# LSTM grid and landmark attention on one core: where the twice-normed rows are added up, and how the first statistics are loaded

## The chip, the cores and the metric

The kernel runs on one core of a Trainium2 chip. The metric is the device time of one execution in microseconds (us), the median over three runs. The engines are PE (TensorE: matmuls and turns by an identity, with PEld its weight loads), DVE (VectorE), ACT (ScalarE), POOL (GpSimd) and SP (SyncE, which issues most DMAs here). Each engine takes its instructions in order.

## The reference, cut to what matters

```
x: 16 images x 64 x 64 cells x 128 features
g = group norm of x over a whole image (32 groups of 4 features)
two-dimensional LSTM over g: cell (i, j) needs h and c of (i-1, j) and (i, j-1)
    f0 = sigmoid(g wf0 + h_up uf0)      f1 = sigmoid(g wf1 + h_left uf1)
    it, ot = sigmoid(..), cp = tanh(g wc + (h_up + h_left) uc)
    c = f0 c_up + f1 c_left + it cp ;   h = ot tanh(c)
x = x + h                                       # tokens t = 4096 rows of 128 per image
attention on layernorm(layernorm(t)): its 64 landmarks are means over 64 successive tokens
    (that is, over one grid row i of an image), of the twice-normed rows
then an output projection, a batch-normed recurrence over tokens, residuals
```

## The kernel before, in words

**group_stats** reads every image of x once (L56, 2 MB each, three buffers, from SP's queue), turns 128x128 blocks on PE (L61), and DVE takes the statistics of each feature over the tokens (L62, L63). Two small matmuls (L68, L75) join the groups, and POOL makes grstd with a power (L28, L29). In front of it in PE's queue are the matrices of the attention's convolution (L637 to L640), which need cb_tm, a DMA from a scratch tensor in DRAM.

**lstm_grid** walks the 127 antidiagonals d of the 64x64 grid: all cells (i, d-i) of one diagonal are independent. Features lie on partitions in the gates; one column is one cell of one image. The 16 images are two halves of 8. A *unit* is a diagonal (up to 32 cells, both halves together, at most 512 columns) or, for diagonals with more cells, one half of it. There are 190 units, and *slot* t of the program works on unit t and, in a software pipeline, on its neighbours:
- load (L182, SP's queue) for unit t+5: x rows in *tiles* of up to 16 cells x 8 images = 128 rows, tokens on partitions
- gate_h for unit t (five gates: L207 on PE, L209 on ACT); gate_x for unit t+1 (L203)
- measure for t-2 (L226, L227 on DVE), then the cell: L288 on DVE, L289 on POOL (forget gate times cell), L290 to L292, tanh L293 on ACT
- turn for t-1: h is turned to tokens (hq, L218) and x is added (L220, into ls_tt); h of unit t is made at L297, and the sum of neighbours for the coming diagonal at L199
- factors for t-2 on POOL (L235 to L241, two of them powers)
- enter for t+2: x is turned to features (xp, L189), mean off (L192 DVE), grstd on (L195 POOL)
- normalise for t-3 (L246 on ACT) writes the twice-normed rows, tokens on partitions, into the upper half of ls_tt; store (L253, SP) writes the rows to DRAM
- collect for t-4: the twice-normed rows are turned back to features (yq, L259) and added into acc, laid out features x grid row x image (L261).

The order on all five engines is the program's own (manual schedule). The tiles of a diagonal are cut from its first cell lo, so the last tile is a partial one. PSUM has 8 banks: five for the gates (z) and one each for xp, hq and yq.

**landmarks** then scales acc by gamma/64 and adds beta (L489), and projects it.

Of the kernel before, what the change touches and what calls it, by code (L numbers as in the profile page):

```python
# [8 lines left out]
F32 = mybir.dt.float32  # L9
# [6 lines left out]
P = 128  # L16


STEPS = 32
HALF = STEPS // 2  # L20
EPS = 1e-5


# [8 lines left out]
def group_stats(nc, tc, x, ident, mhalf, gmean, grstd):  # L32

    B, D0, D1, F = x.shape
    N = D0 * D1
    K = N // P
    GS = 4
    with ExitStack() as ctx:
        cp = ctx.enter_context(tc.tile_pool(name="gs_c", bufs=1))
        ld = ctx.enter_context(tc.tile_pool(name="gs_ld", bufs=3))  # L40
        sp = ctx.enter_context(tc.tile_pool(name="gs_s", bufs=2))
        ps = ctx.enter_context(tc.tile_pool(name="gs_ps", bufs=4, space=PSUM))
        ps1 = ctx.enter_context(tc.tile_pool(name="gs_ps1", bufs=1, space=PSUM))

        avg = cp.tile([P, P], F32, name="gs_avg")
        nc.gpsimd.memset(avg, 1.0 / GS)
        for base, sign in ((0, 1), (GS - 1, -1)):
            nc.gpsimd.affine_select(
                out=avg, in_=avg, compare_op=ALU.is_ge, fill=0.0, base=base,
                pattern=[[-GS * sign, P // GS], [0, GS]], channel_multiplier=sign,  # L50
            )

        mv = cp.tile([P, B, 2], F32, name="gs_mv")
        for b in range(B):
            xb = ld.tile([P, K, F], F32, tag="xb", name="gs_xb")
            nc.sync.dma_start(out=xb, in_=x[b].rearrange("i j f -> (i j) f").rearrange("(p k) f -> p k f", k=K))  # L56
            st = sp.tile([P, K // 4, 6], F32, tag="st", name="gs_st")
            for q in range(K // 4):
                tp = ps.tile([P, 4, P], F32, tag="tp", name="gs_tp")
                for k in range(4):  # L60
                    nc.tensor.transpose(tp[:, k, :], xb[:, 4 * q + k, :], ident)  # L61
                nc.vector.bn_stats(st[:, q, :], tp.rearrange("p k n -> p (k n)"))  # L62
            nc.vector.bn_aggr(mv[:, b, :], st.rearrange("p q s -> p (q s)"))  # L63

        mean = cp.tile([P, B], F32, name="gs_mean")
        nc.vector.tensor_copy(mean, mv[:, :, 0])
        mg = ps1.tile([P, B], F32, tag="mg", name="gs_mg")
        nc.tensor.matmul(mg, avg, mean, start=True, stop=True)  # L68
        nc.vector.tensor_copy(gmean, mg)
        dev = cp.tile([P, B], F32, name="gs_dev")  # L70
        nc.vector.tensor_sub(dev, mean, gmean)
        nc.vector.tensor_mul(dev, dev, dev)
        nc.vector.tensor_add(dev, dev, mv[:, :, 1])
        vg = ps1.tile([P, B], F32, tag="vg", name="gs_vg")
        nc.tensor.matmul(vg, avg, dev, start=True, stop=True)  # L75
        var = cp.tile([P, B], F32, name="gs_var")
        nc.vector.tensor_copy(var, vg)
        inv_std(nc, cp, grstd, var, mhalf, "gs")


def lstm_tiles(nc, cp, shape, w, u, bias):
# [21 lines left out]
    rows = [cp.tile([P, KT, 2 * F + 4], F32, name=f"ls_tt{k}") for k in range(7)]  # L103
    for a in rows:
        nc.vector.memset(a[:, :, F : F + 4], 1.0)
    return wt, ut, bt, hs, cs, rows


def lstm_grid(nc, tc, x, fixed, ident, mhalf, gmean, grstd, t1, acc):

# [6 lines left out]
    T = P // HB  # L119
    NC = D0 * HB  # L120
    KT = NC // P
    AHEAD = 5
    xv = x.rearrange("b i j f -> (i j) b f")
    tv = t1.rearrange("b n f -> n b f")
    with ExitStack() as ctx:
        ld = ctx.enter_context(tc.tile_pool(name="ls_ld", bufs=AHEAD + 4, reuse_waits="tile"))
        wk = ctx.enter_context(tc.tile_pool(name="ls_wk", bufs=2, reuse_waits="tile"))
        sm = ctx.enter_context(tc.tile_pool(name="ls_sm", bufs=4, reuse_waits="tile"))
        ps_z = ctx.enter_context(tc.tile_pool(name="ls_psz", bufs=5, space=PSUM, reuse_waits="tile"))
        ps_t = ctx.enter_context(tc.tile_pool(name="ls_pst", bufs=1, space=PSUM, reuse_waits="tile"))  # L130

        wt, ut, bt, hs, cs, rows = fixed

        class Unit:
            pass
# [1 line left out]
        def unit(t, d, s0, s1):  # L137
# [3 lines left out]
            v.n = v.hi - v.lo  # L141
            v.len = v.n * HB
            v.cols = v.ns * v.len

            runs = [(s, i, min(T, v.hi - i)) for s in range(s0, s1) for i in range(v.lo, v.hi, T)]
            runs = [r for r in runs if r[2] == T] + [r for r in runs if r[2] < T]
            v.tiles = [(k, *r) for k, r in enumerate(runs)]
            whole = sum(r[2] == T for r in runs)
# [7 lines left out]
            hp, hn = hs[(d + 1) % 2], hs[d % 2]  # L156
            before, now = cs[(d + 1) % 2], cs[d % 2]
            v.hu, v.hl, v.ho = part(hp, v.lo), part(hp, v.lo + 1), part(hn, v.lo + 1)
            v.cu, v.cl, v.co = part(before, v.lo), part(before, v.lo + 1), part(now, v.lo + 1)
            v.tt = rows[t % len(rows)]  # L160
            v.z, v.a = {}, {}
# [5 lines left out]

        def span(v, s, i, c):

            return slice((s - v.s0) * v.len + (i - v.lo) * HB, (s - v.s0) * v.len + (i - v.lo + c) * HB)  # L170

        def at(v, s, i, c):
            r = v.d + (D1 - 1) * i
            return slice(r, r + (D1 - 1) * (c - 1) + 1, D1 - 1), slice(s * HB, s * HB + HB)

        def norm(v, a):
            return a[:, v.s0 * HB : v.s1 * HB].rearrange("p (s b) -> p s b", b=HB)[:, :, None, :].to_broadcast([P, v.ns, v.n, HB])

        def load(v):
            v.xt = ld.tile([P, KT, F], F32, tag="xt", name="ls_xt")  # L180
            for k, s, i, c in v.tiles:
                nc.sync.dma_start(out=v.xt[: c * HB, k, :], in_=xv[at(v, s, i, c)])  # L182

        def enter(v):

            xp = ps_t.tile([P, NC], F32, tag="xp", name="ls_xp")
            for k, s, i, c in v.tiles:
                q = c * HB
                nc.tensor.transpose(xp[:, span(v, s, i, c)], v.xt[:q, k, :], ident[:q, :q])  # L189
            v.xn = wk.tile([P, NC], F32, tag="xn", name="ls_xn", bufs=4)[:, : v.cols]  # L190
            a = v.xn.rearrange("p (s c b) -> p s c b", s=v.ns, b=HB)
            nc.vector.tensor_tensor(  # L192
                a, xp[:, : v.cols].rearrange("p (s c b) -> p s c b", s=v.ns, b=HB), norm(v, gmean), ALU.subtract
            )
            nc.gpsimd.tensor_tensor(a, a, norm(v, grstd), ALU.mult)  # L195

# [15 lines left out]
        def turn(v):  # L212

            hq = ps_t.tile([P, KT, P], F32, tag="hq", name="ls_hq")
            for k, s, i, c in v.tiles:
                q = c * HB
                j = (i - v.lo) * HB
                nc.tensor.transpose(hq[:q, k, :], v.ho[:, s - v.s0, j : j + q], ident)  # L218
            for q, k0, k1 in v.parts:
                nc.vector.tensor_add(v.tt[:q, k0:k1, 0:F], hq[:q, k0:k1, :], v.xt[:q, k0:k1, :])  # L220

# [7 lines left out]
        def factors(v):  # L229
# [6 lines left out]
            nc.gpsimd.tensor_scalar(ve[:, 1, :k], var, 1.0 + EPS, EPS * EPS, ALU.mult, ALU.add)  # L236
            nc.gpsimd.tensor_tensor(v.tt[:, 0:k, F + 2], ve[:, 0, :k], mhalf[:, :k], ALU.pow)  # L237
            nc.gpsimd.tensor_tensor(v.tt[:, 0:k, F + 3], ve[:, 1, :k], mhalf[:, :k], ALU.pow)  # L238
            v.nb = sm.tile([P, KT], F32, tag="nb", name="ls_nb")
            nc.gpsimd.tensor_tensor(v.nb[:, :k], mean, v.tt[:, 0:k, F + 3], ALU.mult)  # L240
            nc.gpsimd.tensor_scalar(v.nb[:, :k], v.nb[:, :k], -1.0, None, ALU.mult)  # L241
# [8 lines left out]

        def store(v):
            for k, s, i, c in v.tiles:
                nc.sync.dma_start(out=tv[at(v, s, i, c)], in_=v.tt[: c * HB, k, :])  # L253

        def collect(v):
            yq = ps_t.tile([P, NC], F32, tag="yq", name="ls_yq")
            for k, s, i, c in v.tiles:
                q = c * HB
                nc.tensor.transpose(yq[:, span(v, s, i, c)], v.tt[:q, k, F + 4 :], ident[:q, :q])  # L259
            ar = acc[:, v.lo : v.hi, v.s0 * HB : v.s1 * HB].rearrange("p c (s b) -> p s c b", b=HB)  # L260
            nc.vector.tensor_add(ar, ar, yq[:, : v.cols].rearrange("p (s c b) -> p s c b", s=v.ns, b=HB))  # L261

        units, ready = [], {-1: []}
        for d in range(D0 + D1 - 1):
# [48 lines left out]
        with tc.manual_schedule(  # L313
# [2 lines left out]
                mybir.EngineType.SP,  # L316
            }
        ):
            nc.vector.memset(acc, 0.0)
            for t in range(AHEAD):  # L320
                load(units[t])
            for t in range(2):
                enter(units[t])
            for r in ready[-1]:
# [26 lines left out]
def landmarks(nc, tc, acc, gamma, beta, wqkv, mask, ident, qm, km, pinvT):  # L351
# [19 lines left out]
    with ExitStack() as ctx:  # L371
# [113 lines left out]
        with tc.manual_schedule(  # L485
            engines={mybir.EngineType.PE, mybir.EngineType.DVE, mybir.EngineType.Activation, mybir.EngineType.Pool}
        ):
            for w in range(B // GI):
                nc.vector.tensor_scalar(  # L489
                    xl[w], acc[:, :, images(w)].rearrange("p i b -> p b i"), gm, beta, ALU.mult, ALU.add  # L490
                )
            project_queries(0)
            project_keys(0)
# [904 lines left out]
def kernel(ctx: ExitStack, tc: tile.TileContext, ins: dict, out: bass.AP):  # L1398
# [25 lines left out]
    with tc.tile_pool(name="at_c", bufs=1) as ac, tc.tile_pool(name="at_x", bufs=1) as xp, tc.tile_pool(  # L1424
# [6 lines left out]
        qm = lmk.tile([P, B, 2, D0], F32, name="qm")  # L1431
        km = lmk.tile([P, B, 2, D0], F32, name="km")
        with tc.tile_pool(name="first", bufs=1) as first:
            acc = first.tile([P, D0, B], F32, name="acc")
            gmean = first.tile([P, B], F32, name="gmean")
            grstd = first.tile([P, B], F32, name="grstd")
            lw = [[ins[f"L0_conv_{k}{g}"] for g in GATES] for k in "wub"]
            with tc.tile_pool(name="ls_c", bufs=1) as lc:
                lstm_fixed = lstm_tiles(nc, lc, (B, D0, F), *lw)
                with tc.manual_schedule(engines={mybir.EngineType.SP}):  # L1440
                    group_stats(nc, tc, x, ident, mhalf, gmean, grstd)
                lstm_grid(nc, tc, x, lstm_fixed, ident, mhalf, gmean, grstd, t1, acc)
            rows = [load_rows(nc, xp, t1, 0, g) for g in range(3)]
            landmarks(nc, tc, acc, gamma, beta, wqkv, mask, ident, qm, km, pinvT)
        attention(
# [27 lines left out]
```

## Time and profile before

| | us |
|---|---|
| median of three runs | 4086.14 |
| lowest and highest | 4075.14, 4089.61 |
| profiled execution: its time | 4091.27 |
| its span, first to last instruction | 4089.7 |
| conv matrices, statistics and start of the grid | 0 to 132 |
| the grid, from the first gate_h to the last unit's | 132 to 1517 |
| landmarks, attention, recurrence | from 1529 |

| engine | busy us | share of span |
|---|---|---|
| PE | 3870.2 | 95% |
| DVE | 2983.5 | 73% |
| POOL | 2809.3 | 69% |
| ACT | 2519.4 | 62% |

The busy shares are means over stages with different limits: the second half of the span (attention and recurrence) is not touched by the change. What it touches lies in the first 1530 us, so the profile is read there, window by window. A busy PE is modelled and need not be a PE at its peak; the start times of its instructions tell more. A line of a timeline is: start, duration, engine, source line, operation, tiles, and in brackets the idle time before it with what ended it.

### The profile page before, as it was taken

The page shows a single profiled execution, that of the slowest core. Times are in us where ns is not written, and L with a number is a line of the kernel's source. Part 1 is how long each engine was busy: PE and PEld are TensorE (multiplying, and loading weights), DVE is VectorE, ACT ScalarE, POOL GpSimd, SP SyncE. Part 2 cuts the span into 40 slices and gives each one's busy share as a digit, 9 for nine tenths or more (in the row PEclk, how much of TensorE's full clock was granted, in tenths as well). Part 3 has the DMA queues.
Part 4 walks back from the last instruction along what each step waited for, and adds up shares of the span by engine and source line. Part 5 has one row for each costly group of instructions (what it writes and reads, how often), then busy time and mean ns, then how long its engine had stood idle before and what let it go on. Part 6 is the DMA issues. An engine that isn't in the chain of part 4 may idle for free. (4 is left out here: it accounts for less than half of the span.)

```text
span 4089.7 us, 99565 instructions
## 1 busy us (share of the span) xinstructions
PE 3870.2 (95%) x37526; PEld 2621.9 (64%) x37526; DVE 2983.5 (73%) x7408; ACT 2519.4 (62%) x5101; POOL 2809.3 (69%) x4189
## 2 busy tenths in 40 slices
PE   6899999999999998879999999999999999988697
PEld 4767665555567578846666666666666666655476
DVE  7678777777778775435887878877877787857465
ACT  0366655555566664335777777777767776755597
POOL 0477777777777773317888888888888888877133
PEclk9799999999999989979999999999999999989798
DMA  8122222223233220111333333333333333223799
GB/s 314 61 71 79 77 77 74 80 79 84 75 81 83 70 57 4 39 27 52 94 90 88 88 94 89 88 91 94 92 83 91 93 90 85 83 65 92 235 263 180
DMA packets 493557, 383.85 MB, mean 94 GB/s; under 512 B 35208, under 2 KB 466192, under 8 KB 491024
## 3 DMA queue, kind: packets, MB, share of 16 engines
q1 hardware_dynamic: 471680, 341.17, 28.8%
q0 software_dynamic: 17728, 34.61, 4.7%
q8 instruction: 299, 4.90, 0.5%
q10 hardware_dynamic: 3664, 1.65, 0.1%
q14 instruction: 186, 1.52, 0.1%
HBM read 172.82 MB, written 204.48 MB: 92 GB/s over the span
## 5 line engine op out<-in xcount | busy, mean ns | idle before, releaser
L209 ACT ACTIVATE ls_g<-ls_z,ls_b 128x304 f32<-128x304 f32 (+26 forms) x950 | 510.1, 548 | 401.1 <-PE ls_z L207 364.2
L931 POOL TENSOR_TENSOR at_total<-at_total,at_e 128x512 f32<-128x512 f32 x480 | 611.4, 1274 | 118.3 <-ACT at_e L904 87.2
L203 PE MATMUL ls_z<-ls_xn,ls_w 128*128 128x304 f32 (+26 forms) x1900 | 612.0, 470 | 0.0
L203 PEld LDWEIGHTS ls_z<-ls_xn,ls_w 128*128 128x128 f32 x1900 | 342.7, 197 | 176.0 <-issue 79.5
L798 POOL TENSOR_SCALAR at_T<-at_T,at_nb 128x128 f32<-128x128 f32 x512 | 403.7, 797 | 13.3
L867 DVE TENSOR_REDUCE at_mxq<-at_bank 128x1 f32<-128x512 f32 x512 | 327.7, 683 | 82.9 <-PE at_bank L864 82.6
L207 PE MATMUL ls_z<-ls_hsum,ls_u 128*128 128x304 f32 (+26 forms) x1140 | 372.5, 464 | 0.0
L289 POOL TENSOR_TENSOR ls_g<-ls_g,ls_cell 128x304 f32<-128x304 f32 (+26 forms) x190 | 175.8, 925 | 280.2 <-ACT ls_g L209 250.8
L904 ACT ACTIVATE at_e<-at_bank 128x512 f32<-128x512 f32 x512 | 264.3, 603 | 115.8 <-PE at_bank L898 112.7
L986 DVE TENSOR_REDUCE at_cmx<-at_bank 128x8 f32<-128x512 f32 x512 | 317.4, 683 | 18.5 <-PE at_bank L979 12.7
L1015 ACT ACTIVATE at_eT<-at_bank 128x512 f32<-128x512 f32 x512 | 264.3, 603 | 75.1 <-PE at_bank L1012 75.0
L207 PEld LDWEIGHTS ls_z<-ls_hsum,ls_u 128*128 128x128 f32 x1140 | 214.8, 198 | 128.6 <-issue 78.0
L246 ACT ACTIVATE ls_tt<-ls_tt,ls_nb 128x128 f32<-128x128 f32 (+9 forms) x632 | 261.0, 479 | 4.1 <-POOL ls_nb L241 4.1
L207 PE MATMUL ls_z<-ls_h,ls_u 128*128 128x304 f32 (+26 forms) x760 | 260.3, 466 | 1.7 <-DVE ls_h L297 1.6
L290 DVE TENSOR_TENSOR ls_g<-ls_g,ls_g 128x304 f32<-128x304 f32 (+26 forms) x190 | 98.3, 518 | 195.4 <-POOL ls_g L289 194.2
L237 POOL TENSOR_TENSOR ls_tt<-ls_ve,mhalf 128x4 f32<-128x4 f32 (+2 forms) x190 | 228.5, 1203 | 15.2
L1286 DVE SCALAR_TENSOR_TENSOR rc_y<-rc_w,rc_scale,rc_z 128x256 f32<-128x256 f32 x344 | 155.2, 480 | 108.5 <-PE rc_z L1273 105.7
L1273 PE MATMUL rc_z<-rc_y,rc_vT 128*128 128x256 f32 x688 | 185.4, 406 | 41.6 <-ACT rc_y L1294 29.9
L1067 ACT ACTIVATE at_z<-at_u,at_nb,at_r 128x128 f32<-128x128 f32 x512 | 211.7, 505 | 11.9 <-POOL at_nb L1062 11.9
L238 POOL TENSOR_TENSOR ls_tt<-ls_ve,mhalf 128x4 f32<-128x4 f32 (+2 forms) x190 | 214.6, 1129 | 0.0
L1077 ACT COPY at_fx<-at_bank 128x512 f32<-128x512 f32 x128 | 133.1, 1040 | 126.5 <-DVE wx_stats L1075 100.9
L1267 POOL DMA_DIRECT2D out_dram<-rc_tt x64 | 77.4, 1209 | 189.5 <-ACT rc_tt L1264 186.7
(250 smaller groups left out, 9620.6 us busy)
## 6 DMA issues: line engine op xcount, KB each, us to landing
t<-ls_tt SPq DMA_DIRECT2D x392, 130.0 KB
at_T<-t SPq DMA_DIRECT2D x128, 264.0 KB
gs_xb<-in_x_dram SPq DMA_DIRECT2D x16, 2048.0 KB
at_xh<-t SPq DMA_DIRECT2D x128, 256.0 KB
t<-at_u SPq DMA_DIRECT2D x128, 256.0 KB
out_dram<-at_u SPq DMA_DIRECT2D x128, 256.0 KB
wx<-at_fx SPq DMA_DIRECT2D x128, 256.0 KB
rc_w<-wx SPq DMA_DIRECT2D x64, 512.0 KB
```

Source lines behind the costliest of these rows:

```text
L203: nc.tensor.matmul(v.z[g][:, : v.cols], wt[g], v.xn, start=True, stop=False)
L207: nc.tensor.matmul(view(v, v.z[g]), ut[g], hin, start=False, stop=True)
L209: nc.scalar.activation(a[:, : v.cols], v.z[g][:, : v.cols], AF.Tanh if g == 4 else AF.Sigmoid, bias=bt[g])
L237: nc.gpsimd.tensor_tensor(v.tt[:, 0:k, F + 2], ve[:, 0, :k], mhalf[:, :k], ALU.pow)
L238: nc.gpsimd.tensor_tensor(v.tt[:, 0:k, F + 3], ve[:, 1, :k], mhalf[:, :k], ALU.pow)
L246: nc.scalar.activation(v.tt[:q, k, F + 4 :], v.tt[:q, k, 0:F], AF.Identity, bias=v.nb[:q, k : k + 1], scale=v.tt[:q, k, F + 3 : F + 4],)
L798: nc.gpsimd.tensor_scalar(x[:, c, :], x[:, c, :], gr.nbt[:, 0, c : c + 1], gr.nbt[:, 1, c : c + 1], ALU.mult, ALU.subtract)
L867: nc.vector.tensor_reduce(gr.im.mxq[:, n : n + 1, gr.g], gr.s[n], AX.X, ALU.max)
L904: nc.scalar.activation(gr.e[:, n].rearrange("p c m -> p (c m)"), s[n], AF.Exp)
L931: nc.gpsimd.tensor_tensor(total, total, e[:, :, c, :], ALU.add)
L986: nc.vector.tensor_reduce(gr.mx[:, n].rearrange("p j c -> p c j"), gr.s[n].rearrange("p (c j m) -> p c j m", c=C, j=2), AX.X, ALU.max)
L1015: nc.scalar.activation(gr.eT[:, n], s[n], AF.Exp)
```

## The change

- collect no longer turns anything: it adds the twice-normed rows, tokens on partitions, into acc, which is now laid out token row x half x block of 16 grid rows x feature. One DVE instruction per part of a unit replaces the yq turns and the old addition. landmarks turns acc once, eight 128x128 blocks, before L489.
- For that a token row must always stand for the same grid row, so tiles are cut at multiples of 16 cells (base) instead of from lo. From diagonal 64 on, the first tile of a unit can then hold dead rows in front. Their x rows are set to zero on POOL before the load (one memset per such tile), and their second factor is multiplied by a column of a 0/1 matrix (later) on POOL. The other tiles are whole. The number of tiles and DMAs stays as it was.
- The bank of yq goes to the gates: six z banks.
- group_stats loads quarters of an image (512 KB, eight buffers, 64 DMAs) instead of whole images (three buffers, 16 DMAs).
- The pool of x rows (ls_ld) is opened ahead of group_stats, and the rows of the first five units are loaded from ACT's queue. The memset of acc moves ahead too.

```
 group_stats:
-            xb = ld.tile([P, K, F], F32, tag="xb", name="gs_xb")
-            nc.sync.dma_start(out=xb, in_=x[b]...)
+                if q % 2 == 0:
+                    xb = ld.tile([P, 8, F], F32, tag="xb", name="gs_xb")
+                    nc.sync.dma_start(out=xb, in_=rows[:, 4 * q : 4 * q + 8, :])
...
 unit:
+            v.base = v.lo // T * T
-            runs = [... for i in range(v.lo, v.hi, T)]
+            runs = [... for i in range(v.base, v.hi, T)]
...
 load:
+                rows, cells = inner(v, i, c)
+                if rows.start:
+                    nc.gpsimd.memset(v.xt[:, k, :], 0.0)
-                nc.sync.dma_start(out=v.xt[: c * HB, k, :], in_=xv[at(v, s, i, c)])
+                eng.dma_start(out=v.xt[rows, k, :], in_=xv[cells, s * HB : s * HB + HB])
...
 factors:
+            for j, s, i, c in v.tiles:
+                if i < v.lo:
+                    f = v.tt[:, j, F + 3 : F + 4]
+                    nc.gpsimd.tensor_tensor(f, f, later[:, v.lo - i : v.lo - i + 1], ALU.mult)
...
 collect:
-            yq = ps_t.tile([P, NC], F32, tag="yq", name="ls_yq")
-            for k, s, i, c in v.tiles:
-                q = c * HB
-                nc.tensor.transpose(yq[:, span(v, s, i, c)], v.tt[:q, k, F + 4 :], ident[:q, :q])
-            ar = acc[:, v.lo : v.hi, v.s0 * HB : v.s1 * HB].rearrange(...)
-            nc.vector.tensor_add(ar, ar, yq[:, : v.cols].rearrange(...))
+            for q, k0, k1 in v.parts:
+                i = v.tiles[k0][2] // T
+                a = acc[:q, v.s0 : v.s1, i : i + (k1 - k0) // v.ns, :]
+                y = v.tt[:q, k0:k1, F + 4 :].rearrange("p (s t) f -> p s t f", s=v.ns)
+                nc.vector.tensor_tensor(a, a, y, ALU.add)
...
 start of the grid:
-                load(units[t])
+                load(units[t], nc.scalar)
...
 landmarks:
+                p = ps.tile([P, W, P], F32, tag="bank", name="lm_bank")
+                for i in range(W):
+                    nc.tensor.transpose(p[:, i, :], acc[:, w, i, :], ident)
```

## The prediction

> **What bounds the kernel now.** I read the stages first (busy time by window), then the PE timeline inside one unit of the grid, then POOL's waits by stage, last the front. Columns of the first view: window, its length, busy us (instructions) of PE, weight load, DVE, ACT, POOL, then granted clock, DMA share, GB/s.
>
> ```profile
> core 0: us, PE busy (x) PEld busy (x) DVE busy (x) ACT busy (x) POOL busy (x), PEclk, DMA share, GB/s
> ...
> 34.00:119.00 85.00, 76.19 (x512) 55.36 (x512) 84.14 (x154) 1.28 (x1) 0.00 (x0) 1.00 0.83 328
> 119.00:132.00 13.00, 4.46 (x19) 4.00 (x19) 2.12 (x11) 0.00 (x0) 3.72 (x4) 0.54 0.02 6
> ...
> 552.00:837.00 285.00, 285.00 (x994) 158.07 (x993) 213.16 (x560) 164.57 (x310) 201.94 (x250) 1.00 0.29 78
> ...
> 1145.00:1321.00 176.00, 176.00 (x784) 127.87 (x783) 140.82 (x430) 113.96 (x243) 137.01 (x214) 1.00 0.30 81
> ...
> 1446.00:1512.00 66.00, 64.33 (x427) 57.27 (x426) 57.81 (x222) 45.98 (x135) 57.27 (x127) 0.98 0.24 66
> ```
>
> The statistics (34 to 119) run at DVE's pace, 84 of 85 us. The grid (132 to 1512) shows PE full, and the timeline says this is real: gates of 416 columns start every 0.35 us, and the three groups of turns follow without a gap:
>
> ```profile
> 604.80 0.60 PE L218 MATMUL ls_hq<-ident,ls_h 128*128 128x128 f32 x4
> 605.24 0.67 PE L189 MATMUL ls_xp<-ident,ls_xt 128*128 128x128 f32 x4
> 605.84 0.71 PE L259 MATMUL ls_yq<-ident,ls_tt 128*128 128x128 f32 x4
> 606.48 0.62 PE L203 MATMUL ls_z<-ls_xn,ls_w 128*128 128x416 f32 x1
> ```
>
> Start to start, the hq turns take 0.44, the xp turns 0.60, the yq turns 0.64 us of an 8.8 us unit. But POOL and DVE are not far behind. All that POOL idles is its wait at L289 for the forget gate (us in total, times, longest), here in 552 to 837, 1145 to 1321 and 1446 to 1512:
>
> ```profile
> POOL ls_g L289 <- ACT ls_g L209: 68.2, 31, 2.5
> ```
> ```profile
> POOL ls_g L289 <- ACT ls_g L209: 28.0, 27, 1.5
> ```
> ```profile
> POOL ls_g L289 <- ACT ls_g L209: 1.7, 5, 0.6
> ```
>
> So POOL has over 2 us to spare in each unit of the first, 1.0 in the second, and nothing in the last, where POOL, not PE, sets the pace.
>
> **The change, part by part.**
>
> *yq turns removed (632).* Busy time of L259's tile by window is 11.65 (173 to 336), 17.73 (336 to 552), 19.73, 22.64 (837 to 1145), 14.65, 8.89 (1321 to 1446) and 7.40. The pipeline's last 0.1 us of each unit overlaps the next gate (0.71 against 0.64), so PE's queue loses 9.2, 14.4, 16.6, 19.1, 12.0, 7.3 and 5.8 us. *Whole tiles from diagonal 64 on:* xp turns with a remainder tile take 0.60, four whole ones as hq 0.44; summed over those units about 4.4, 3.9 and 2.3 us more in 837 to 1145, 1145 to 1321 and 1321 to 1446. PE alone would gain about 95 us. What is late next is POOL's L289 and DVE's L290 behind it.
>
> *collect on DVE.* L261 (median 0.52, one input in PSUM) becomes one addition of 256, 384 or 512 elements, plus one for a remainder below diagonal 64. By L290 (0.59 at 416 elements) and L291 (0.42 at 256) that is 0.42, 0.56 or 0.69, and 0.2 for the remainder. DVE gets 0.1 to 0.3 us more in a unit; from diagonal 64 on L220 pays half of it back (two instructions of 0.74 become one of 0.69). DVE's waits at L290 and L288 are 33.7 us in 33 units of 336 to 552: this hides it.
>
> *What that addition does to POOL.* Both inputs now lie in SBUF. The rows:
>
> ```profile
> 604.69 0.59 DVE L290 TENSOR_TENSOR ls_g<-ls_g,ls_g 128x416 f32<-128x416 f32 x1 [1.25 <-POOL ls_g L289]
> ```
> ```profile
> 604.74 0.63 POOL L235 TENSOR_SCALAR ls_ve<-ls_tt 128x4 f32<-128x4 f32 x1
> ```
> ```profile
> 1496.09 0.22 POOL L235 TENSOR_SCALAR ls_ve<-ls_tt 128x2 f32<-128x2 f32 x1
> ```
> ```profile
> 599.96 0.55 DVE L261 TENSOR_TENSOR acc<-acc,ls_yq 128x392 f32<-128x392 f32 x1
> ```
> ```profile
> 600.35 1.07 POOL L195 TENSOR_TENSOR ls_xn<-ls_xn,grstd 128x416 f32<-128x416 f32 x1
> ```
>
> L235 is 0.41 us longer when it starts under L290, and ends just behind it; L195 under the old L261 is as long as anywhere. The Trainium skill ("SBUF — State Buffer", section Who interferes with whom) has the rule: a DVE instruction with two SBUF inputs contends with a GpSimd instruction that reads SBUF, not with one that only writes it, and the later one waits for the other's end. It speaks against this change: the addition now holds back L240, L241 and L195, which start 0.1 to 0.3 us into it today. Each is then some 0.2 to 0.5 us later in a unit (length of the addition, less that start, less 0.13 for what overlaps). By the rule POOL loses 0.3 to 0.4 in most units; without it the sum below would be 16 us better. The row agrees, so I take the rule.
>
> *Dead rows.* 120 tiles (one in most units of diagonals 64 to 94, two after) get a memset of 128x128 on POOL and a multiplication of 128x1. POOL's memsets of that size in the prologue took 0.20; the nearest row to the other is L240, 0.19, and 0.28 to the next start. I take 0.47 a tile, 0.94 a unit after diagonal 94; ends 0.3 (the memset covered by handover) and 1.3 (both held back 0.41 as L235 was). SP's load now waits for the memset; behind it are only the stores of L253, some 4 us later, and SP issues 5.4 of 8.8 us, so this is free while the memset is less than that late. The first reader of a load is five units away.
>
> *Units' balance.* Gain is the smaller of PE's saving and POOL's idle less what it is given:
> - 132 to 336: +7. The narrow units up to 205 have no POOL idle: lock costs 1; the rest gets PE's saving.
> - 336 to 552: idle 1.0, lock 0.37, PE 0.44: the first few units fall short, +11.
> - 552 to 837: idle 2.3: all, +17. 837 to 1145: idle 2.1, lock 0.42, dead 0.47: all, +23.
> - 1145 to 1321: idle 0.95 without handover, less 0.3 and 0.47: 0.15 in each of 27, +4 (PE offers 16).
> - 1321 to 1446: idle 1.6, less 0.37 and 0.94: +2.5.
> - 1446 to 1512: no idle, 16 units, 0.2 and up to 0.94 more: -14 (the last five load nothing any more).
> Sum: 51 us less. The last units' factors chain pays 1.5 more behind 1512.
>
> *Sixth z bank:* nothing; the fifth gate function ends at 605.6, before the next x gates start at 606.48. The first to refill are long read.
>
> *Front.* PE's first work waits for cb_tm, which shares the DMA engines with the first three images:
>
> ```profile
> 24.07 0.77 PE L637 MATMUL cb_t<-cb_turn,cb_tm 128*128 128x128 f32 x2 [24.07 <-DMA cb_tm<-cb_flat]
> ```
> ```profile
> 127.31 0.58 PE L189 MATMUL ls_xp<-ident,ls_xt 8*128 8x8 f32 x2 [5.21 <-DMA ls_xt<-in_x_dram]
> ...
> 129.71 1.46 PE L203 MATMUL ls_z<-ls_xn,ls_w 128*128 128x16 f32 x6
> ```
>
> Three images are 6.3 MB; eight quarters are 4.2. At 0.42 MB a us, what the DMA view shows in most slices from 7 to 22 us, the queue is dry 5 us earlier: -5 (ends 0, if cb_tm needs its 17 us anyway, and -9). 48 more issues of 0.33 us on SP lie under the stage. DVE's 128 statistics are not shortened; a stage that DVE fills gains nothing from quarters. acc's memset only moves on DVE. Then x rows of the first units are loaded by ACT's queue (10 issues, ACT idle) long before: the wait to 127.31 goes, and the first gates follow grstd (125.74) and one L192 and L195 at about 126.3 instead of 129.71: -3.4. The clock is at half there either way (0.54 in 119 to 132).
>
> *End.* Eight turns at half clock, some 0.25 each, mostly under the wait for the last store to land (1528.7), and xl is then read from PSUM at a like price: +0.5, ends 0 and 2.
>
> Sum: -51 - 5 - 3.4 + 1.5 + 0.5 = -57. The profiled execution took 4091.3 (span 4089.7), 5 above the median 4086.1; the difference is taken from the median: 4029.
>
> **The rivals.**
> A. *PE gets nearly all.* The lock costs nothing (67 by the same balance) and the memsets slip into handovers (4 more): with front and end, 6.4, that is -77: 4009. For it: busy PE everywhere. Against: L235's row.
> B. *POOL becomes the bound from diagonal 64 on: slower.* If memset and multiplication are both held back behind DVE (1.3 to 1.4 a tile), POOL's idle of 837 to 1446 is overdrawn: by the same balance, at 1.4, 837 to 1145 gives 9, 1145 to 1321 -22, 1321 to 1446 -20, the narrow end -39; the rest gives 35, front and end 6.4: 31 slower, 4117. It breaks even near 1.1 a tile. Against: the memset only writes.
> C. *Little comes through.* POOL pays 0.9 a tile, by the same balance: the grid gains 14, with front and end 20: 4066, or some us more if cb_tm gains nothing (4071). Against it stands the 0.20 of the prologue's memsets.
>
> **How the numbers follow.** Likeliest 4029 (0.57), A 0.21, C 0.13, B 0.09. A difference of 0.5% (20 us) is about what a measurement of this kernel can tell. Faster 0.78, same 0.13, slower 0.09. The range runs from A with its best front (3996) to C (4072).
>
> **What would show it.** Right: units near 600 at 8.1 us instead of 8.8; L195 lengthened under L261's successor; POOL without idle after 1145; units of the narrow end longer by 0.6 to 1.0; cb_tm at about 19; first gates 8 us earlier. Wrong: units near 1200 shortened by PE's full 0.6 to 0.9 (A), units near 900 not shortened (B), cb_tm still at 24.

## The result, and the profile after

| us | before | after |
|---|---|---|
| median (lowest to highest) | 4087.88 (4075.14 to 4095.67), 4 runs | 4020.82 (4017.51 to 4027.51), 4 runs |
| profiled execution, its span | 4091.27, 4089.7 | 4021.31, 4019.8 |

The ratio is 0.9841, with a 95% interval of 0.9813 to 0.9869: 67 us less. In the two profiles the grid's last unit starts its first gate_h at 1516.6 and at 1445.3, so 71.3 us are won before that point, and 1.4 are lost behind it.

Most lines moved; the ones used below, before to after: load L182 to L200, with the new memset L199; xp turn L189 to L207; L192 to L210; L195 to L214; gate_x L203 to L222; gate_h L207 to L226; hq turn L218 to L237; factors L235 to L238 now L254 to L257, with the new multiplication L261; L240, L241 to L263, L264; addition of collect L261 to L284; L289 and L290 to L312 and L313.

To see where the 71 us are, one grid has to be laid on the other. A unit is the same stretch of the grid in both, so the table counts units (0 to 189 in the order of the program) and takes a stage from the first gate_h of one unit to that of another. "My step" is the prediction's amount for the window nearest to the stage; their ends lie up to 8 us apart.

| stage | before | after | gain | my step |
|---|---|---|---|---|
| up to the first gate_h | 131.9 | 123.4 | 8.5 | 8.4 |
| units 0 to 32 | 204.7 | 194.0 | 10.7 | 7 |
| 32 to 63 | 207.4 | 196.7 | 10.6 | 11 |
| 63 to 95 | 290.1 | 273.4 | 16.7 | 17 |
| 95 to 130 | 310.8 | 288.1 | 22.7 | 23 |
| 130 to 157 | 176.5 | 169.1 | 7.4 | 4 |
| 157 to 173 | 128.1 | 122.8 | 5.3 | 2.5 |
| 173 to 189, the narrow end | 67.2 | 77.8 | -10.6 | -14 |

The stages' busy times after the change (window, its length, busy us and instructions of PE, weight load, DVE, ACT, POOL, then granted clock, DMA share, GB/s) are the statistics, the wait for the grid, units 63 to 95, units 130 to 157, and the narrow end:

```profile
core 0: us, PE busy (x) PEld busy (x) DVE busy (x) ACT busy (x) POOL busy (x), PEclk, DMA share, GB/s
26.00:111.00 85.00, 69.59 (x501) 56.46 (x497) 83.30 (x154) 0.00 (x0) 0.32 (x2) 0.98 0.93 356
111.00:123.40 12.40, 5.47 (x34) 4.80 (x33) 5.39 (x16) 1.28 (x1) 3.72 (x4) 0.74 0.01 4
...
514.00:787.50 273.50, 273.50 (x895) 148.45 (x894) 225.65 (x605) 168.81 (x320) 218.49 (x264) 1.00 0.30 82
...
1075.60:1244.80 169.20, 165.00 (x705) 119.57 (x704) 140.61 (x404) 105.14 (x241) 156.11 (x271) 1.00 0.31 84
...
1367.50:1445.30 77.80, 63.28 (x387) 55.52 (x387) 58.95 (x226) 46.15 (x139) 69.86 (x186) 0.95 0.20 56
```

PE is still full in units 63 to 95, with 895 instructions recorded, but it is no longer full at the end (165.0 of 169.2, then 63.3 of 77.8). POOL's busy time has grown from 57.3 in 66 us to 69.9 in 77.8. The timeline of PE inside one unit shows what went: two groups of turns, and then the next gates.

```profile
570.22 2.26 PE L226 MATMUL ls_z<-ls_hsum,ls_u 128*128 128x416 f32 x6
572.31 0.60 PE L237 MATMUL ls_hq<-ident,ls_h 128*128 128x128 f32 x4
572.75 0.68 PE L207 MATMUL ls_xp<-ident,ls_xt 128*128 128x128 f32 x4
573.35 3.76 PE L222 MATMUL ls_z<-ls_xn,ls_w 128*128 128x416 f32 x10
```

POOL's waits (us in total, times, longest) have shrunk from 70.4 us (68.2 of them for ACT) to 38.9 in units 63 to 95:

```profile
POOL ls_g L312 <- ACT ls_g L228: 25.6, 20, 1.5
POOL ls_g L312 <- DMA t<-ls_tt: 13.3, 10, 1.5
```

From unit 130 to 157 the same view lists no wait of POOL at all, where it had 28.0 us before. PE, which never waited for POOL in a group of the old page, now does so in L222's: 8.0 us over the kernel.

```profile
L222 PE MATMUL ls_z<-ls_xn,ls_w 128*128 128x304 f32 (+26 forms) x1900 | 607.2, 468 | 8.6 <-POOL ls_xn L214 8.0
```

The front came out as two separate gains. The first turn of cb_tm starts 5.5 us earlier (18.61 instead of 24.07), and the x turn ahead of the first gates (that of unit 1; the one of unit 0 is not among the records) now waits for DVE's L210 and no longer for a DMA:

```profile
18.61 0.76 PE L662 MATMUL cb_t<-cb_turn,cb_tm 128*128 128x128 f32 x2 [9.09 <-DMA cb_tm<-cb_flat]
```
```profile
120.84 0.39 PE L207 MATMUL ls_xp<-ident,ls_xt 16*128 16x16 f32 x2 [3.91 <-DVE ls_xn L210]
121.19 2.32 PE L222 MATMUL ls_z<-ls_xn,ls_w 128*128 128x16 f32 x10
```

### The profile page after: what moved, and what is told of

The parts are those of the page before. It is cut to its first block, busy times and chain, and to the rows that moved or that the text cites. A ratio compares the mean times of both kernels' runs of the same rounds, so it can differ in the third digit from the quotient of the medians.

```text
span 4019.8 us, 98633 instructions
## 1 busy us (share of the span) xinstructions
PE 3774.1 (94%) x36902; PEld 2552.7 (64%) x36902; DVE 3017.4 (75%) x7408; ACT 2494.2 (62%) x5101; POOL 2910.2 (72%) x4431
## 5 line engine op out<-in xcount | busy, mean ns | idle before, releaser
L228 ACT ACTIVATE ls_g<-ls_z,ls_b 128x304 f32<-128x304 f32 (+26 forms) x950 | 489.3, 545 | 234.3 <-PE ls_z L226 200.6
L222 PE MATMUL ls_z<-ls_xn,ls_w 128*128 128x304 f32 (+26 forms) x1900 | 607.2, 468 | 8.6 <-POOL ls_xn L214 8.0
L222 PEld LDWEIGHTS ls_z<-ls_xn,ls_w 128*128 128x128 f32 x1900 | 340.6, 196 | 190.7 <-issue 85.1
L226 PE MATMUL ls_z<-ls_hsum,ls_u 128*128 128x304 f32 (+26 forms) x1140 | 371.3, 463 | 0.0
L226 PEld LDWEIGHTS ls_z<-ls_hsum,ls_u 128*128 128x128 f32 x1140 | 213.5, 196 | 128.6 <-issue 76.9
L226 PE MATMUL ls_z<-ls_h,ls_u 128*128 128x304 f32 (+26 forms) x760 | 260.7, 466 | 17.4 <-DVE ls_h L320 17.2
L316 ACT ACTIVATE ls_g<-ls_cell 128x304 f32<-128x304 f32 (+26 forms) x190 | 93.3, 491 | 284.0 <-DVE ls_cell L315 281.0
L312 POOL TENSOR_TENSOR ls_g<-ls_g,ls_cell 128x304 f32<-128x304 f32 (+26 forms) x190 | 182.5, 960 | 96.7 <-ACT ls_g L228 66.9
L256 POOL TENSOR_TENSOR ls_tt<-ls_ve,mhalf 128x4 f32<-128x4 f32 (+2 forms) x190 | 224.5, 1181 | 15.2
L313 DVE TENSOR_TENSOR ls_g<-ls_g,ls_g 128x304 f32<-128x304 f32 (+26 forms) x190 | 98.5, 518 | 159.7 <-POOL ls_g L312 155.5
L226 PEld LDWEIGHTS ls_z<-ls_h,ls_u 128*128 128x128 f32 x760 | 141.6, 196 | 110.5 <-issue 51.0
```

Of the source, the lines that this page charges most:

```text
L222: nc.tensor.matmul(v.z[g][:, : v.cols], wt[g], v.xn, start=True, stop=False)
L226: nc.tensor.matmul(view(v, v.z[g]), ut[g], hin, start=False, stop=True)
L228: nc.scalar.activation(a[:, : v.cols], v.z[g][:, : v.cols], AF.Tanh if g == 4 else AF.Sigmoid, bias=bt[g])
```

## The experiments

The work behind the grid is the same in all kernels, yet from the last unit's gate_h to the end of the span it took between 2551 us (no_sum) and 2579 us (quarters) in the profiled executions. Totals of single kernels therefore scatter by more than most parts of this change are worth, and the parts are read from the stages. Within the grid, from unit 7 to 173, a stage that an edit doesn't touch repeats within 0.7 us, and mostly within 0.1. The narrow end does so less well, because the granted clock falls to half around its last two units, in each profile at another moment: those two took 8.7 us in the changed kernel and 9.3 before, at half clock for the most part, and 5.6 to 7.2 us in four runs that kept full clock longer (turns_back, no_dead, mask_add, mask_pool).

**quarters: only the load in quarters, on the old grid.**

```diff
-        ld = ctx.enter_context(tc.tile_pool(name="gs_ld", bufs=3))
+        ld = ctx.enter_context(tc.tile_pool(name="gs_ld", bufs=8))
...
+                if q % 2 == 0:
+                    xb = ld.tile([P, 8, F], F32, tag="xb", name="gs_xb")
+                    nc.sync.dma_start(out=xb, in_=rows[:, 4 * q : 4 * q + 8, :])
```

> The kernel before, with the group statistics loaded in quarters of an image (eight buffers) and nothing else changed. If the front's gain comes from the shorter queue ahead of cb_tm and the rest from the early x rows (my steps: 5 and 3.4 us), the first cb transpose moves from 24 to about 19 us, the first gate_h from 131.9 to about 127, and the total is 5 us less. If the queue does not matter and the x rows carry all of it, cb moves too but the first gate_h stays within 1 us of 131.9. The grid itself (132 to 1517) should not move by more than 1 us, unless the earlier start also moves the moment at which TensorE's clock comes back to full; then units 0 to 7 are up to 4 us shorter.

The first cb transpose moved to 20.20, the last turn of the statistics from 117.6 to 113.1, and the first gate_h from 131.9 to 126.9: 5.0 us. Units 0 to 7 took 33.1 instead of 37.3 us. All stages from unit 7 to 173 stood still. The median was 4085.5, ratio 0.9992 (0.9983 to 1.0001): the 9 us that the grid's start won in the profile are not seen in the whole. The part behind the grid was 6 us longer in this profile; why the medians of 20 and 45 runs lie only 2.4 us apart is open.

**whole_front: quarters, and the first x rows loaded early on ACT's queue.**

```diff
-        def load(v):
+        def load(v, eng=nc.sync):
...
-            nc.vector.memset(acc, 0.0)
             for t in range(AHEAD):
-                load(units[t])
+                load(units[t], nc.scalar)
...
-            with tc.tile_pool(name="ls_c", bufs=1) as lc:
+            with tc.tile_pool(name="ls_c", bufs=1) as lc, tc.tile_pool(name="ls_ld", bufs=AHEAD + 4) as ld:
+                nc.vector.memset(acc, 0.0)
```

> The kernel before with both parts of the front: quarters, and the x rows of the first five units loaded early on ACT's queue (pool of the rows opened ahead of the statistics, accumulator cleared earlier). The grid is the old one. Theory: first gate_h at about 123.4 as in the changed kernel, units 0 to 7 at 33 us instead of 37.3, so 12 to 13 us less in all, near 0.997 of the time before. Rival (the 4 us in units 0 to 7 belong to the new grid, not to the start): units 0 to 7 stay at 37, total 8 to 9 us less. What is left to the grid is the measured 70 us less this.

First gate_h at 121.4, units 0 to 7 in 33.4 us, the last unit 13.75 us earlier; 4076.0, ratio 0.9977 (0.9968 to 0.9985), which is 6 to 13 us of the whole. So in the profiles the front is worth nearly 14 us and the new grid the other 57 or 58. What shortens units 0 to 7 is the clock. From 121 to 160 us, in the kernel before, with quarters, and with the whole front, the windows read (the granted clock is the third number from the end):

```profile
121.00:160.00 39.00, 31.89 (x146) 29.37 (x147) 12.81 (x65) 11.38 (x38) 14.18 (x34) 0.50 0.05 15
```
```profile
121.00:160.00 39.00, 36.28 (x187) 33.32 (x187) 16.53 (x79) 14.92 (x50) 15.41 (x43) 0.57 0.06 18
```
```profile
121.00:160.00 39.00, 38.70 (x213) 35.58 (x214) 20.51 (x96) 18.80 (x62) 19.57 (x52) 0.63 0.05 15
```

The granted clock in the trace is at half from 119.9 to 171.1 before (51.2 us), from 117.1 to 154.6 in quarters (37.5) and from 115.8 to 149.9 here (34.1). Before, full clock comes inside unit 7; here, inside unit 5. All twelve profiles go the same way: where full clock is back 27 to 29 us after the first gate_h, units 0 to 7 take 32.9 to 33.4 us, where it takes 32 us (z_five, after_again), 34.6, and where it takes 39.2 (before), 37.3.

**turns_back: the new grid with the yq turns issued again, read by nobody.**

```diff
-        ps_z = ctx.enter_context(tc.tile_pool(name="ls_psz", bufs=6, space=PSUM, reuse_waits="tile"))
+        ps_z = ctx.enter_context(tc.tile_pool(name="ls_psz", bufs=5, space=PSUM, reuse_waits="tile"))
...
+            yq = ps_t.tile([P, NC], F32, tag="yq", name="ls_yq")
+            for k, s, i, c in v.tiles:
+                q = c * HB
+                nc.tensor.transpose(yq[:, span(v, s, i, c)], v.tt[:q, k, F + 4 :], ident[:q, :q])
```

> The changed kernel with the yq turns of collect issued again on TensorE (their result is read by nobody; five z banks as before). Theory (the grid's gain is TensorE's time): units 32 to 157 go back by nearly what they gained, about 14, 17, 20 and 9 us in units 32-63, 63-95, 95-130 and 130-157, the units 157 to 173 by 4, the narrow end by 1 or 2; about 60 to 65 us in all, 4080. Rival 1 (whole tiles and the shorter turns of x carry a good part): only 30 to 40 us go back. Rival 2 (the addition from SBUF instead of PSUM or the sixth bank is what helped DVE): less than 20 us go back.

4075.9, ratio 0.9969 (0.9958 to 0.9981). Against the changed kernel the stages lost 7.2 (16 to 32), 10.6, 16.7, 15.3 (95 to 130), 2.7, 3.2, and the narrow end won 1.7 (nearly all of it in the last two units, at a higher clock): 54 us. The last unit comes 53 us later, less than the 60 to 65 expected and well above what the rivals said. Units 16 to 95 went back to the old times to 0.1 us, so all of their gain is the turns. The timeline has them back between the x turns and the gates; in units of four tiles (95 to 129) every slot is 0.44 us longer, in the next ones, of three, 0.33:

```profile
592.08 0.67 PE L207 MATMUL ls_xp<-ident,ls_xt 128*128 128x128 f32 x4
592.68 0.71 PE L283 MATMUL ls_yq<-ident,ls_tt 128*128 128x128 f32 x4
593.32 3.76 PE L222 MATMUL ls_z<-ls_xn,ls_w 128*128 128x416 f32 x10
```

In units 95 to 130, 7.4 us of the gain stayed. They belong to the whole tiles, which shorten three things: from the start of one group to that of the next, the x turns take 14.6 us in all instead of 16.9, the yq turns 15.3 instead of 18.5, and the gates behind them 2.0 less. In unit 114, before and here, the yq turns start 0.60 and 0.44 us behind the x turns:

```profile
1014.60 0.67 PE L189 MATMUL ls_xp<-ident,ls_xt 128*128 128x128 f32 x4
1015.20 0.75 PE L259 MATMUL ls_yq<-ident,ls_tt 128*128 128x128 f32 x4
```
```profile
1000.29 0.60 PE L207 MATMUL ls_xp<-ident,ls_xt 128*128 128x128 f32 x4
1000.73 0.60 PE L283 MATMUL ls_yq<-ident,ls_tt 128*128 128x128 f32 x4
```

The first rival said that the whole tiles and the shorter x turns carry a good part. They carry these 7.4 us, and at most 4.7 and 2.1 more in units 130 to 157 and 157 to 173, where POOL takes part of what PE saves.

**z_five: five z banks instead of six.**

```diff
-        ps_z = ctx.enter_context(tc.tile_pool(name="ls_psz", bufs=6, space=PSUM, reuse_waits="tile"))
+        ps_z = ctx.enter_context(tc.tile_pool(name="ls_psz", bufs=5, space=PSUM, reuse_waits="tile"))
```

> The changed kernel with five z banks instead of six. My step said the sixth bank is worth nothing: every stage within 0.5 us of the changed kernel. Rival (without the yq turns the x gates of the next unit come so early that they would wait for a bank, so the sixth is part of the gain): units 63 to 130 are 0.1 to 0.3 us longer each, 7 to 20 us in all.

4023.1, ratio 0.9855 (0.9838 to 0.9871). Every stage from unit 7 on is within 0.5 us of the changed kernel; units 0 to 7 took 34.6, under a half clock of 41.0 us. In the grid the sixth bank is worth nothing.

**no_dead: the work on dead rows left out.**

```diff
-            v.xt = ld.tile([P, KT, F], F32, tag="xt", name="ls_xt")
+            v.xt = ld[v.t % len(ld)]
-                if rows.start:
-                    nc.gpsimd.memset(v.xt[:, k, :], 0.0)
...
-            for j, s, i, c in v.tiles:
-                if i < v.lo:
-                    f = v.tt[:, j, F + 3 : F + 4]
-                    nc.gpsimd.tensor_tensor(f, f, later[:, v.lo - i : v.lo - i + 1], ALU.mult)
...
+                for a in ld:
+                    nc.vector.memset(a, 0.0)
```

> The changed kernel without the work on dead rows: the row buffers are fixed tiles cleared once, the memset of a tile and the multiplication by later are left out (so dead rows are added into the sums: part of the computation is changed). Theory (POOL is the bound from about unit 130 on, and the dead rows are what takes its time): the narrow end 173-189 goes from 77.8 to 66-69 us, 157-173 by 2 to 4 less, 130-157 by 2 to 4 less (TensorE is at 165 of 169 us there), 63-130 by at most 3 less; 13 to 20 us in all, about 4003. Rival (the lock under the addition, or DVE itself, sets the narrow end): under 6 us in all, narrow end above 74.

4007.9, ratio 0.9811 (0.9795 to 0.9827). Units 7 to 130 did not change (by 0.7 us at most), though dead tiles begin at unit 96: there PE is the bound, and POOL's extra work is free. Units 130 to 157 went from 169.1 to 161.4 (all of it from unit 144 on), 157 to 173 from 122.8 to 119.4, and the narrow end from 77.8 to 65.6: 23.3 us, more than I had expected here. Not all of this is the dead rows. Of the 12.2 us of the narrow end 2.6 lie in the last two units, which kept full clock here (it fell at 1431.4, behind the last unit's first gate_h at 1429.8) and had lost it in the changed kernel (at 1438.0). turns_back has the dead rows and kept full clock there, and is 1.5 us faster than the changed kernel in these two units; by that the dead rows cost about 22 us. The stretch ahead of them, from unit 173 to unit 187, went from 69.0 to 59.4, against 57.8 before. The first gate_h came 7.2 us later: 5.2 of that go with where the fixed buffers lie (see mask_pool), and the rest may be their clears on DVE, which no run has separated. The narrow end now reads:

```profile
1364.30:1429.80 65.50, 57.21 (x386) 52.03 (x386) 59.50 (x220) 45.25 (x137) 57.89 (x127) 1.00 0.24 66
```

**no_sum: the addition of collect left out, dead rows kept.**

```diff
         def collect(v):
-            for q, k0, k1 in v.parts:
-                ...
-                nc.vector.tensor_tensor(a, a, y, ALU.add)
+            pass
```

> The changed kernel without the addition of collect (the accumulator stays zero: part of the computation is left out); everything else, dead rows too, as in the changed kernel. Theory (the addition of two SBUF operands holds back one POOL instruction of a unit by 0.3 to 0.4 us, which counts only where POOL is the bound): units up to 143 do not move; units 144 to 157 are 0.3 to 0.4 us shorter each, 4 to 5 us; units 169 to 173 one to two us in all; the narrow end 173-189 0.2 to 0.35 each, 3 to 6 us; 8 to 13 us in all, about 4010. Rival (the lock is absorbed, it only moves the wait from one POOL instruction to another): under 2 us. A second rival (DVE is the bound of the wide units 32 to 63, where it had no idle time in the profile): those units get 0.3 us shorter each, 9 us more.

3999.5, ratio 0.9793 (0.9776 to 0.9809). The stages from unit 7 on won 1.0, 0.0, 3.1 (32 to 63), 0.0, 0.0, 6.4 (130 to 157), 2.4 and 3.3: 16.2 us in all. The theory's place is right: units 63 to 143 stand still, units 144 to 156 win 0.3 to 0.7 each. Its size was not: it said 8 to 13 us. The second rival is not borne out: DVE had hardly any idle time in units 32 to 63, and yet they win 3.1 us and not 9, spread over units 36 to 55. The lock, that is, a POOL instruction held back by the addition, is seen in unit 149, first in the changed kernel (POOL, and DVE at the same time), then without the addition:

```profile
1197.19 1.04 POOL L257 TENSOR_TENSOR ls_tt<-ls_ve,mhalf 128x3 f32<-128x3 f32 x1
1198.31 0.58 POOL L261 TENSOR_TENSOR ls_tt<-ls_tt,ls_later 128x1 f32<-128x1 f32 x1
1198.97 0.19 POOL L263 TENSOR_TENSOR ls_nb<-ls_tt 128x3 f32<-128x3 f32 x1
```
```profile
1198.30 0.55 DVE L284 TENSOR_TENSOR acc<-acc,ls_tt 128x384 f32<-128x384 f32 x1
```
```profile
1187.85 1.04 POOL L257 TENSOR_TENSOR ls_tt<-ls_ve,mhalf 128x3 f32<-128x3 f32 x1
1188.96 0.19 POOL L261 TENSOR_TENSOR ls_tt<-ls_tt,ls_later 128x1 f32<-128x1 f32 x1
1189.23 0.19 POOL L263 TENSOR_TENSOR ls_nb<-ls_tt 128x3 f32<-128x3 f32 x1
```

L261 starts with the addition, 1198.31 and 1198.30, and ends with it, 1198.89 and 1198.85: 0.58 us for a column that takes 0.19 alone. This is what the Trainium skill ("SBUF — State Buffer", section Who interferes with whom) says of a DVE instruction with two SBUF inputs and a POOL instruction that reads SBUF. Which POOL instruction is held turns on hundredths of a microsecond. As the units shrink, L261's start moves from 0.13 us ahead of the addition's (unit 131) to 0.07 behind it (unit 156). Up to unit 144, where it is 0.03 ahead, L261 takes 0.19 and L263 is held, by 0.19 us in the end. From unit 145, where it is 0.02 ahead, L261 is held, by 0.42 us at first, and L263 is free. In unit 142 (POOL, then DVE):

```profile
1154.57 0.19 POOL L261 TENSOR_TENSOR ls_tt<-ls_tt,ls_later 128x1 f32<-128x1 f32 x1
1154.84 0.38 POOL L263 TENSOR_TENSOR ls_nb<-ls_tt 128x3 f32<-128x3 f32 x1
```
```profile
1154.62 0.55 DVE L284 TENSOR_TENSOR acc<-acc,ls_tt 128x384 f32<-128x384 f32 x1
```

**no_memset: fixed row buffers and no memset, the multiplication kept.**

```diff
-            v.xt = ld.tile([P, KT, F], F32, tag="xt", name="ls_xt")
+            v.xt = ld[v.t % len(ld)]
-                if rows.start:
-                    nc.gpsimd.memset(v.xt[:, k, :], 0.0)
```

> The changed kernel with the row buffers as nine fixed tiles and without the memset of a tile with dead rows (a dead row then holds an older, finite row; its factor is still multiplied by zero). It splits the 23.3 us that the dead rows cost in units 130 to 189 (7.7, 3.4 and 12.2 by the run without them). By my step (memset 0.20, multiplication 0.27 a tile) the memset carries 40%: 3 us in 130-157, 1.4 in 157-173, 4 in 173-189 (11 units still load there). Theory now (the memset's start to start is 0.17, the multiplication is the one that is held back behind the addition): memset 2.4, 1 and 3.7, so 7 us in all, about 4014. Rival (the memset delays the row load behind it, SP's queue and the store): over 12 us.

4020.3, ratio 0.9834 (0.9811 to 0.9856). The narrow end won 4.1 us, about as expected (0.4 of it in unit 187, where the clock differs), but units 130 to 157 only 0.4 and 157 to 173 only 0.1. The timeline of unit 149 says why, and units 144 to 152 all show the same 0.13 to 0.16 us. Without the memset POOL's forget gate (L310 here, L312 in the changed kernel) starts while DVE's L309, with two SBUF inputs, is running, and takes 1.04 us; in the changed kernel the memset (L199), which only writes, lies under that DVE instruction and the gate takes 0.89. These are POOL and DVE without the memset, then POOL of the changed kernel:

```profile
1204.93 1.04 POOL L310 TENSOR_TENSOR ls_g<-ls_g,ls_cell 128x296 f32<-128x296 f32 x1
```
```profile
1204.69 0.60 DVE L309 TENSOR_TENSOR ls_g<-ls_g,ls_cell 128x296 f32<-128x296 f32 x1
```
```profile
1200.20 0.21 POOL L199 MEMSET ls_xt<- 128x128 f32 x1
1200.37 0.89 POOL L312 TENSOR_TENSOR ls_g<-ls_g,ls_cell 128x296 f32<-128x296 f32 x1
```

**mask_add: dead rows without an instruction of their own.**

```diff
-            v.xt = ld.tile([P, KT, F], F32, tag="xt", name="ls_xt")
+            v.xt = ld[v.t % len(ld)]
-                if rows.start:
-                    nc.gpsimd.memset(v.xt[:, k, :], 0.0)
...
+            dead = v.lo - v.base
+            if dead:
+                nc.gpsimd.tensor_tensor(
+                    ve[:, 1, :k].rearrange("p (s t) -> p s t", s=v.ns), var.rearrange("p (s t) -> p s t", s=v.ns),
+                    later[:, dead, : v.ns, : k // v.ns], ALU.add,
+                )
+            else:
+                nc.gpsimd.tensor_scalar(ve[:, 1, :k], var, 1.0 + EPS, EPS * EPS, ALU.mult, ALU.add)
```

> The changed kernel with dead rows that cost no instruction: nine fixed row buffers without a memset, and in units with dead rows the variance gets a table added (EPS squared, or 1e30 in dead rows, which makes their factor 1e-15) in place of the tensor_scalar with the same constant; the constant factor 1/sqrt(1 + EPS), five in a million, is left out in those units. Theory: as in the run without the work on dead rows, 7.7, 3.4 and 12.2 us less in units 130-157, 157-173 and 173-189, without that run's longer front (its clears on DVE, 4.8 us): 3996 to 4000. Rival: the tensor_tensor that replaces the tensor_scalar is dearer on POOL by 0.2 or more and gives a third back: 4005.

3996.7, ratio 0.9791 (0.9774 to 0.9807). Units 130 to 157, 157 to 173 and the narrow end won 7.7, 3.7 and 11.8 us. The rival's dearer instruction did not appear: the tensor_tensor takes 0.20 us in unit 180, as long as the tensor_scalar in the changed kernel (0.19). The first gate_h came at 128.3, as late as in no_memset (128.7).

**mask_pool: the same, with the row buffers in a pool of their own; after_again: the changed kernel beside it.**

```diff
-            with tc.tile_pool(name="ls_c", bufs=1) as lc:
-                ld = [lc.tile([P, D0 * B // 2 // P, F], F32, name=f"ls_xt{k}") for k in range(AHEAD + 4)]
+            with tc.tile_pool(name="ls_c", bufs=1) as lc, tc.tile_pool(name="ls_ld", bufs=1) as lx:
+                ld = [lx.tile([P, D0 * B // 2 // P, F], F32, name=f"ls_xt{k}") for k in range(AHEAD + 4)]
```

> The kernel of mask_add with one thing moved: the nine fixed row buffers lie in a pool of their own, opened where the changed kernel opens its pool of rows, and not among the tiles of the grid, whose space was used before. In mask_add ACT's queue could issue the first x rows only at 38.8 us, in the middle of the statistics (in the changed kernel from 3.9 us on), and the first gate_h came at 128.3 instead of 123.4. Theory (that late issue is what cost the front): x rows issued before 16 us again, first gate_h at 121.5 to 123.5, grid as in mask_add, so about 5 us less than mask_add and 23 to 24 less than the changed kernel: 3990 to 3998. Rival (the front only scatters from run to run by 5 us): first gate_h near 128 again, no difference to mask_add.

> The changed kernel once more, on the same chip as mask_pool. Theory: ratio to the kernel before 0.983 to 0.985; first gate_h at 121.7 to 123.4 and units 0 to 7 in 33 us; every stage of the grid within 0.5 us of its first profile. Rival (the gain at the start is scatter): units 0 to 7 at 37 us as in the kernel before.

mask_pool: 3999.0, ratio 0.9779 (0.9753 to 0.9805). after_again: 4021.1, ratio 0.9829 (0.9805 to 0.9852). ACT's queue issues the first x rows at 38.77 in mask_add and at 3.95 here:

```profile
38.77 6.94 ACTq L199 DMA_DIRECT2D ls_xt<-in_x_dram  x10
```
```profile
3.95 0.65 ACTq L199 DMA_DIRECT2D ls_xt<-in_x_dram  x2
```

The first gate_h is back at 123.1, and the last unit's is 24.9 us ahead of the changed kernel's. The total lies just above the 3990 to 3998 expected, and the medians of mask_pool and mask_add do not differ; those 5 us are a reading of the profiles alone. PE is the bound again up to unit 173:

```profile
1075.30:1236.80 161.50, 161.50 (x705) 119.21 (x704) 147.69 (x405) 113.12 (x243) 142.17 (x216) 1.00 0.33 89
1236.80:1355.80 119.00, 118.96 (x445) 73.36 (x443) 101.05 (x266) 77.89 (x157) 97.10 (x128) 1.00 0.29 78
1355.80:1420.40 64.60, 57.03 (x387) 52.08 (x387) 59.20 (x221) 45.41 (x139) 57.34 (x128) 1.00 0.25 67
```

after_again repeated the stages from unit 7 to 173 to 0.1 us. Its first gate_h came at 124.2, its units 0 to 7 took 34.6 and its narrow end took 80.5 us, the latter at a granted clock of 0.89: the clock fell to half at 1432.9, before the grid was done. These two stages carry 2 to 3 us of scatter.

## Why the prediction was right, step by step

It said 57 us less in the profile; the span lost 69.9 and the median 67, inside the range. By its own steps:

- **yq turns removed:** right in mechanism and size. Units 32 to 130 won 50.0 us where the steps had 51. turns_back shows that the turns are all of it up to unit 95. From 95 to 130 the yq turns took 18.5 us from start to start, where the step had 19.1.
- **Whole tiles:** right that they help, but mis-sized. The x turns became 2.3 us shorter in units 95 to 130, and not 4.4; 2.0 us that the step did not have came from the gates behind them.
- **The lock:** the row and the rule were right. The addition holds back what the prediction named, each in other units: L264 (0.45 us in unit 70, 0.23 without the addition), L263 (0.64 and 0.20 in unit 110), L214 (1.41 and 1.17 in unit 160), and from unit 145 also the new L261. Its worth in the sum, 16 us, agrees with the 16.2 that the grid wins without the addition, but this agreement is partly luck: no_sum takes DVE's own time away with it, and in units 144 to 152 its win is cut off at what PE has to give.
- **Dead rows at 0.47 us a tile:** right in the narrow end, where taking them out wins 0.83 to 0.88 us in units 179 to 183, which have two such tiles and still load. The two memsets carry 0.3 of that.
- **Balance of units 130 to 173: the step that failed most.** It put one price on POOL for a whole stage, 0.77 and 1.31 us a unit (lock and dead rows), set it against POOL's idle, and got gains of 4 and 2.5. The measured ones are 7.4 and 5.3. Units 130 to 143 and 158 to 168 won 0.29 to 0.63 us each, as much as without dead rows, so PE set their pace. Units 144 to 156 won 0.17 each, as the step had it (0.15). POOL's idle before was much the same in both parts, so what it was given differs: idle less gain leaves at most 0.48 us a unit in units 140 to 143 (4.1 us of idle, 2.2 won) and 0.85 in units 144 to 156 (13.2 and 2.2). About half of the difference is seen under no_sum: the addition holds L263 by 0.19 us in the former and L261 by some 0.4 in the latter, and the switch, between units 144 and 145, is where POOL falls behind. The other half is open. Without dead rows units 130 to 157 win 7.7 us and without the addition 6.4; these do not add up, because PE has only 7.7 us to give there.
- **Narrow end, -14 predicted, -10.6 measured:** right in mechanism. From unit 173 to unit 187, ahead of the fall of the clock, the loss is 11.2 us. Taking out the dead rows wins 9.6 there, taking out the addition 3.4 (0.24 a unit, sized at 0.2). The two together exceed the loss by 1.8, and about as much, 1.7 us, POOL had idled there before; the step took this as nothing.
- **Front, 5 and 3.4:** the last turn of the statistics came 4.1 us earlier and the rest of the way to the first gate_h is 4.4 shorter. quarters alone gave 5.0.
- **"The clock is at half there either way":** this term was mis-sized. It is at half in both, but 17 us shorter after (34.1 against 51.2), a term that the sum put at nothing. Units 0 to 7 won 4.4 us, and 3.9 of that come with the front alone (whole_front).
- **Sixth bank nothing, end nearly nothing:** z_five agrees on the first; the 1.4 us lost behind the grid are within that part's scatter.

Of the rivals, A (the lock costs nothing, memsets slip into handovers) fits units 130 to 143 but failed on units 144 to 156, which won at most 0.36 us each; without dead rows they show that PE had 0.6 to 0.8 to give. B needed 1.1 us a tile, and a tile costs 0.43. C failed with cb_tm and with units 63 to 130, which won everything PE had to give.

## What to carry to other kernels

Costs that are added to one engine are to be laid out in order on its timeline before they are summed. What a lock costs depends on which instruction meets it, 0.19 us or 0.4 here, and hundredths of a microsecond in a start decided which it was; and removing a write-only instruction can give nothing when the next reader walks into the lock in its place. Work that is moved off the bound engine is worth what the next engine's idle time allows, unit by unit, so where the work shrinks towards the end of a loop the small helpers decide: here some 22 us went to a clear and a mask, and a table that is added in place of a constant, with buffers that need no clear, took them back. And where a buffer lies decides when its first load may start: the same nine tiles allocated in used space were loaded at 38.8 us instead of 4, and the first gate_h came 5.2 us later.

## What the runs showed of the hardware

Between the statistics and the first gates PE has little to do (in the changed kernel it is busy for 5.5 of the 12.4 us from 111.0 to 123.4), and the granted clock falls to half. How long it stays there is a whole number of steps in the traces: 34.1 us in eight of the profiles here, 37.5 in quarters and after_again, 41.0 in z_five, 51.2 before. The shortest stretch of half clock in the traces is 3.41 us (from 35.1 to 38.5 us in the changed kernel), and the four lengths are 10, 11, 12 and 15 times that. A busy PE didn't end it at once: in the changed kernel PE was busy for 32.4 of the 32.9 us of units 0 to 7 and still had the half clock for the first 27.7 of them, until 151.1. What picks the number isn't settled: quarters and the kernel before both waited 5.2 us for x rows, and one took 37.5, the other 51.2.
